# One step apart: an output projection, a diagonal product and a module gate moved inside a selective-scan loop

## The chip, the core and the metric

The kernel runs on one core of a Trainium2 chip, in one launch. The metric is the device time in microseconds (us). The engines are named as in the profile: PE is the matmul engine (PEld is its weight load), DVE the vector engine, ACT the scalar engine, POOL the GpSimd engine, and SP the engine that issues most DMAs.

## What is computed

The whole program is two layers over an input of 4 x 256 x 32 x 32: a hybrid layer (four small Mamba modules, a gated convolution, attention), then attention and a mixture of 16 experts. Only the Mamba part of the first layer is touched here. In short form, for each batch element and each of four groups of 64 channels:

```
xc  = layernorm(x)                        # 64 channels of this group, 1024 positions
u,z = xc @ inw.T ; u = silu(conv(u))      # 128 channels each
dt  = softplus(...) ; h_t = exp(dt*A)*h + dt*u*B ; y_t = <h_t, C_t>     # 16 states per channel
y   = y + u * D
xm  = (y * silu(z)) @ outw.T + skip_scale * xc
...
g   = sigmoid(two small convolutions over all 256 channels of xm)       # one gate per group
xg  = g * xm
```

`u * D`, `skip_scale * xc`, the product with `outw` and the gate `g` are the pieces that the change moves.

## The kernel before

There are 4 batch elements `b` and 4 modules `nb`, so 16 pairs, and I call each pair a block `n = 4b + nb`. A block holds 128 channels x 16 states = 2048 recurrences of 1024 positions. They are processed in 16 steps `j`, 128 recurrences at a time, so the scan loop has 256 steps `t = 16n + j` (plus 4 to drain). All work is written into one loop over `t`, and inside it the order of the source is the order on every engine: nothing is rescheduled. The position of a piece of work is therefore the step in which the loop calls it. The change's own short description says "block" for what is called a step here.

In every step the loop emits, in this order:

- DVE: `dBu * B` (L876, in place in PSUM) and the scan itself (L879). They form the recurrence's input and output `hs`.
- POOL: `hs * C` (L880).
- In step 3, ACT copies the finished `pY` of the block before (`gated`, L485).
- PE: `select(t+2)` (L817) spreads `dt*u` for two steps later into one of **two** `dBu` PSUM buffers. It can run only when scan `t` has finished with that buffer, and DVE needs it two steps later.
- PE: `add_up(t-3)` sums `hs * C` over the states into `pY`. In the first two and last two positions of a block this is L828 (4 matmuls). Between them, every second step does two steps at once with L835 (8 matmuls that run in pairs). It also holds the product `u * D` as a matmul with a diagonal (`ddiag`, L841), one half of the columns in each of two steps. `add_up` also releases `hs`, which has six buffers.
- SP and ACT: fetch `dt` of four steps ahead (L805), and the exponential of it for three steps ahead (`decay`, L810).
- Then the pieces of the block's surroundings, each in its own step: the front of the next block (`project` L403, `silu` L407, `project_dt` L414, `exps`, `rest` L425/L426, `log`, `dt_out` L432 to L435, `part1`/`part2` L439 to L445, the two `spread`s L461/L463, DMAs `parts_out` L449 and `turn` L456), `times_gate` of the block before (L488, POOL), `project_out` (L498/L499), `store` (L504, ACT), `gate` (L476/L478), and the module gate of the batch element before (`module_gate`, L513 to L530).

All of these surrounding pieces pass through **one** PSUM buffer of 128 x 1024, called `mm` (the function `big()`), so each waits until the one before has been read out of it. In step order `mm` belongs to `project_dt`, `exps` and `log` (steps 0 to 5, released by L432 on DVE in step 5), `spread(0)` (6), `spread(1)` (7), `project_out` (8) to `store` (9), `gate` (9), in some blocks `module_gate` (10), and `project` and `silu` of the next block (11 to 15).

A matmul in float32 appears as two instructions of 512 columns; a half of 512 columns is therefore two, a full width of 1024 is four. `project_out` adds two products in one accumulation: `sdiag` (the diagonal of `skip_scale`) times `xc`, with the 64 rows of this module as contraction, and the output weights of the two modules of a pair times `u`, with 128 rows. Only the 64 output rows of this module are stored.

Of the kernel before, what the change touches and what calls it, by code (L numbers as in the profile page):

```python
# [13 lines left out]
ALU = mybir.AluOpType  # L14
# [4 lines left out]
N = HH * WW  # L19
# [4 lines left out]
NB, DM, DIN, DS, DTR, K = 4, 64, 128, 16, 4, 4  # L24
# [3 lines left out]
DB, XL = P // DS, K - 1  # L28
# [288 lines left out]
def body(tc, g, out):  # L317
    nc = tc.nc
    act, mm = nc.scalar.activation, nc.tensor.matmul
    ts, tt, stt = nc.vector.tensor_scalar, nc.vector.tensor_tensor, nc.vector.scalar_tensor_tensor  # L320
    HALVES = (slice(0, 512), slice(512, 1024))
# [4 lines left out]
    with pool("const", 1) as cp, pool("dram", 1, space=bass.MemoryType.DRAM) as drp, contextlib.ExitStack() as late:  # L326
# [16 lines left out]
        def V(name, j=0, n=1):  # L343
            return vec[:, VOFF[name] + j : VOFF[name] + j + n]
# [19 lines left out]
        XM = []  # L364
        for b in range(B):
            t = xmp.tile([P, CT, XL + N + 1], F32, tag=f"xm{b}", name=f"xm{b}")
# [4 lines left out]
        order = [(nb, b) for b in range(B) for nb in range(NB)]  # L371
        NBLK = NJ * len(order)
        with pool("mconst", 1) as mc, pool("front", 1) as fp, pool("dts", 2, space=bass.MemoryType.DRAM) as dsp, pool(
# [8 lines left out]
            sdiag = mc.tile([P, P], F32, tag="sdiag", name="sdiag")  # L382

            def block(nb, b):
                q0 = (nb % 2) * DM
                return slice(q0, q0 + DM), XM[b][q0 : q0 + DM, nb // 2]

            def big():
                return mps.tile([P, N], F32, tag="mm", name="mm")
# [90 lines left out]
            def gated(n):  # L480
                u, pY, sz = (state[n][k] for k in ("u", "pY", "sz"))
                if n == len(order) - 1:
                    tt(u, pY, sz, ALU.mult)
                else:
                    nc.scalar.copy(u, pY)  # L485

            def times_gate(n):
                nc.gpsimd.tensor_tensor(state[n]["u"], state[n]["u"], state[n]["sz"], ALU.mult)  # L488

            def project_out(n):  # L490


                nb, b = order[n]
                rows_out, xb = block(nb, b)
                po = state[n]["po"] = big()
                two = m_out[:, nb // 2 * 2 : nb // 2 * 2 + 2].rearrange("p n d -> p (n d)")
                for h in HALVES:
                    mm(po[:, h], sdiag[rows_out, :], xb[:, XL + h.start : XL + h.stop], start=True, stop=False)  # L498
                    mm(po[:, h], two, state[n]["u"][:, h], start=False, stop=True)  # L499

            def store(n):
                nb, b = order[n]
# [3 lines left out]
            def module_gate(b, step):  # L506

                q12 = late_gate[0]  # L510
                if step == 0:
                    if b == 0:
                        nc.gpsimd.memset(q12, 0.0)  # L513
                    p = big()
                    for h in HALVES:
                        for k in range(CT):
                            mm(p[:96, h], qdw[:, k, :], XM[b][:, k, XL + h.start : XL + h.stop], start=k == 0, stop=k == CT - 1)
                    for j in range(3):
                        rows_j = slice(32 * j, 32 * j + NB)
                        act(  # L520
                            q12[rows_j, 2 - j : 2 - j + N], p[rows_j], AF.Identity,
                            bias=V("qdw_b")[rows_j] if j == 1 else 0.0, scale=1.0,
                        )
                else:
                    k, t = step - 1, late_gate[1]
                    p = big()
                    for h in HALVES:
                        mm(p[:, h], qpw[:, k * P : (k + 1) * P], q12[:, 1 + h.start : 1 + h.stop], start=True, stop=True)
                    act(t, p, AF.Sigmoid, bias=V("qpw_b", k), scale=1.0)
                    nc.gpsimd.tensor_tensor(XM[b][:, k, XL : XL + N], XM[b][:, k, XL : XL + N], t, ALU.mult)  # L530

            late_gate = []
            state = {}
            with pool("scan", 6) as sp, pool("yps", 1, space=PSUM) as yps, pool("dps", 2, space=PSUM) as dps, pool("lnA", 1) as wp:
# [10 lines left out]
                for b in range(B - 1, B):  # L545
                    t = wp.tile([P, CT, N], F32, tag=f"xs{b}", name=f"xs{b}")
# [251 lines left out]
                def which(t):  # L798

                    return t % NJ // 8 * 8 + t % 2 * 4 + t % 8 // 2  # L800

                def fetch(t):
                    if t < NBLK:
                        dAs[t] = sp.tile([P, N], F32, tag="dA", name="dA", bufs=5)
                        nc.sync.dma_start(out=dAs[t], in_=state[t // NJ]["ds"][which(t)].unsqueeze(0).to_broadcast([DS, DB, N]))  # L805

                def decay(t):
                    if t < NBLK:
                        c = order[t // NJ][0] * NJ + which(t)
                        act(dAs[t], dAs[t], AF.Exp, scale=aneg[:, c : c + 1])  # L810

                def select(t):
                    if t < NBLK:
                        j = which(t)
                        dBus[t] = dps.tile([P, N], F32, tag="dBu", name="dBu")
                        for h in HALVES:
                            mm(dBus[t][:, h], pick[:, j % 4], state[t // NJ]["U"][:, j // 4, h], start=True, stop=True)  # L817

                def add_up(t):
                    if not 0 <= t < NBLK:  # L820
                        return
                    r, p, j = state[t // NJ], t % NJ, which(t)
                    if p == 0:
                        r["pY"] = yps.tile([P, N], F32, tag="y", name="pY")
                    if not 2 <= p < 14:
                        hs = hss.pop(t)
                        for h in HALVES:
                            mm(r["pY"][:, h], strip[:, P - DB - j * DB : 2 * P - DB - j * DB], hs[:, h], start=p == 0, stop=p == NJ - 1)  # L828
                    elif p % 2:

                        two = {which(u): hss.pop(u) for u in (t - 1, t)}
                        for h in HALVES:
                            for c, hs in two.items():
                                q, i = c // 4, c % 4
                                mm(  # L835
                                    r["pY"][32 * q : 32 * q + 32, h], strip[:, P - DB - i * DB : P - i * DB + 32 - DB], hs[:, h],
                                    start=False, stop=False,
                                )
                    if p in (1, 2):
                        h = HALVES[p - 1]  # L840
                        mm(r["pY"][:, h], ddiag[:, order[t // NJ][0]], r["u"][:, h], start=False, stop=False)  # L841

                fronts = [front(n) for n in range(1, len(order))]
# [26 lines left out]
                with tc.manual_schedule():  # L870
                    for t in range(NBLK + 4):
                        n, j = t // NJ, t % NJ
                        if t < NBLK:
                            r = state[n]
                            dBu = dBus.pop(t)
                            tt(dBu, dBu, r["B"], ALU.mult)  # L876

                            hs = hss[t] = sp.tile([P, N], F32, tag="hs", name="hs")
                            nc.vector.tensor_tensor_scan(hs, dAs.pop(t), dBu, 0.0, ALU.mult, ALU.add)  # L879
                            nc.gpsimd.tensor_tensor(hs, hs, r["C"], ALU.mult)  # L880
                        if j == 3 and n > 0:
                            gated(n - 1)
                        select(t + 2)
                        add_up(t - 3)
                        fetch(t + 4)
                        decay(t + 3)
                        for ahead in (1, 2):
                            if n + ahead < len(order):
                                for i, step in fronts[n + ahead]:
                                    if i == j - (ahead - 1) * NJ:  # L890
                                        step()
                        for i, step in behind:
                            if i == t:
                                step()
                        if 0 < n < len(order) and j == 4:
                            times_gate(n - 1)
                        if n > 0 and j == (8 if n < len(order) else 3):
                            project_out(n - 1)
                        if n > 0 and j == (9 if n < len(order) else 3):
                            store(n - 1)  # L900
                        if n < len(order) and j == 9:
                            gate(n)
                        if n >= NB and j == 10 and n % NB < 3:
                            module_gate(n // NB - 1, n % NB)

# [10 lines left out]
        with pool("sets", 1) as wp, pool("work", 1) as kp, pool("ps2", 1, space=PSUM) as ps:  # L918
# [988 lines left out]
            for i in range(B * NT + 2):  # L1907
                b, unit = i // NT, (i - 2) // HT
# [25 lines left out]
        with pool("fin", 3) as fp, pool("rows", 1) as yp, pool("pfin", 4, space=PSUM) as pf:  # L1934
# [5 lines left out]
            for u in range(2 * B):  # L1940
                b, half = u // 2, u % 2
# [20 lines left out]
```

## Time and profile before

| what | us |
|---|---|
| median of 3 runs | 3153.95 (3152.73 to 3158.89) |
| the profiled execution, its own time | 3144.65 |
| its span, first to last instruction | 3142.9 |
| end of the first and of the last scan, from the span's start | 103.0 and 1114.5 |
| DVE busy between 115 and 1115 us | 905.8 |
| PE busy there | 822.2 |
| POOL busy there | 777.5 |
| ACT busy there | 625.5 |

The profiled execution is 9.3 us below the median of the timed runs, so a sum over its rows is a difference to be taken from either, not an absolute time. The scan loop is about a third of the program. What follows (attention, routing, experts) needs the loop's result: the first of it starts in the trace right after the last `store`. The granted PE clock over the span is 0.939 of full speed.

In timelines a row is: start in us, duration in us, engine, line, operation, output<-inputs, shape, number of instructions merged, and in brackets the idle time of the engine before the row with what ended it. In the table of waits a row is: who waited <- for whom: total us, times, longest us.

### The profile page before, as it was taken

Reading aid. Unit: us, or ns where it says so; the run is one execution under the profiler, and the core shown is the slowest. Engines: PE = TensorE matmul, PEld = TensorE weight load, DVE = VectorE, ACT = ScalarE, POOL = GpSimd, SP = SyncE. Lnnn points to the kernel's source line nnn. Section 1 sums busy time; section 2 is a strip of 40 time slices with the busy share of each in tenths; the row PEclk is TensorE's granted clock in tenths of the full one; section 3 lists DMA queues with packets and bytes.
Section 4 is the critical chain, followed back from the end, with each engine's and each line's share of the span. In section 5 each row is a group of like instructions: output and inputs, shape, how many; then the busy total and the mean of one; then the engine's idle time right before and its main releaser. Section 6 shows DMA issues by size and latency. Waiting matters only on the chain. (4 is left out here: it accounts for less than half of the span.)

```text
span 3142.9 us, 38694 instructions
## 1 busy us (share of the span) xinstructions
PE 2741.2 (87%) x15244; PEld 1555.1 (49%) x15244; DVE 2033.9 (65%) x2324; ACT 1531.9 (49%) x2090; POOL 1289.5 (41%) x806
## 2 busy tenths in 40 slices
PE   6788888888888779999889899989879999899996
PEld 3322222222222225555545555555545666789996
DVE  5799988989989965655785496567365555511112
ACT  3666656666667414455744673576443333211111
POOL 0687877778768710000010010001024434666662
PEclk8799999999999889999989999999989999899998
DMA  3576666656756620000000000000000002456445
GB/s 132 136 176 166 173 159 165 167 153 173 178 153 164 169 87 1 1 1 1 28 1 1 28 1 1 1 15 1 14 1 7 14 14 78 124 148 168 90 125 165
DMA packets 92872, 265.50 MB, mean 84 GB/s; under 512 B 18182, under 2 KB 36086, under 8 KB 89360
## 3 DMA queue, kind: packets, MB, share of 16 engines
q1 hardware_dynamic: 64000, 198.46, 23.6%
q0 software_dynamic: 26512, 60.35, 7.5%
q10 hardware_dynamic: 2176, 4.19, 0.3%
q8 instruction: 121, 1.98, 0.3%
q14 instruction: 63, 0.52, 0.1%
HBM read 291.70 MB, written 42.80 MB: 106 GB/s over the span
## 5 line engine op out<-in xcount | busy, mean ns | idle before, releaser
L880 POOL TENSOR_TENSOR hs<-hs,bc 128x1024 f32<-128x1024 f32 x256 | 600.9, 2357 | 178.6 <-DVE hs L879 176.8
L879 DVE TENSOR_TENSOR_SCAN hs<-dA,dBu 128x1024 f32<-128x1024 f32 x256 | 585.5, 2287 | 45.5 <-PE pY L835 15.6
L1170 DVE TENSOR_REDUCE nm<-s 128x1 f32<-128x1024 f32 x256 | 301.5, 1219 | 187.4 <-PE s L1165 186.6
L1175 ACT ACTIVATE pr<-s,nm 128x1024 f32<-128x1024 f32 x256 | 285.2, 1115 | 234.9 <-DVE nm L1170 232.7
L1189 PE MATMUL k<-const,pr 128*128 128x128 f32 x2048 | 298.8, 289 | 81.0 <-ACT pr L1175 47.9
L876 DVE TENSOR_TENSOR dBu<-dBu,bc 128x1024 f32<-128x1024 f32 x256 | 310.6, 1213 | 50.9 <-PE dBu L817 50.4
L1239 POOL TENSOR_TENSOR b<-b 128x1024 f32<-128x1024 f32 (+1 forms) x15 | 30.3, 2019 | 761.5 <-ACT b L1235 751.8
L810 ACT ACTIVATE dA<-dA,aneg 128x1024 f32<-128x1024 f32 x256 | 285.9, 1144 | 106.2 <-DMA dA<-ds 97.2
L1189 PEld LDWEIGHTS k<-const,pr 128*128 128x128 f32 x2048 | 230.1, 145 | 182.2 <-ACT pr L1175 77.8
L1165 PE MATMUL s<-b,b 32*128 32x512 f32 x1024 | 286.6, 653 | 1.7 <-ACT pr L1175 1.7
L817 PE MATMUL dBu<-U,pick 96*128 96x512 bf16 x512 | 160.6, 396 | 138.2 <-DVE hs L879 137.7
L1195 ACT COPY pT<-k 128x512 f32<-128x512 f32 x320 | 172.8, 594 | 139.5 <-PE k L1189 137.6
L1837 PE MATMUL s<-pT,b 128*128 128x128 f32 x1920 | 233.8, 279 | 6.2 <-DMA b<-we,intse 5.6
L1837 PEld LDWEIGHTS s<-pT,b 128*128 128x128 f32 x1920 | 229.1, 194 | 12.4 <-issue 3.5
L835 PE MATMUL pY<-hs,const 128*32 128x512 f32 x768 | 222.5, 709 | 0.0
L817 PEld LDWEIGHTS <-pick 96*128 96x128 bf16 x512 | 40.2, 98 | 322.0 <-issue 174.7
L1841 DVE TENSOR_TENSOR pT<-pT,s 128x512 f32<-128x512 f32 x72 | 49.3, 685 | 227.2 <-ACT pT L1840 227.2
L1195 DVE COPY pT<-k 128x512 f32<-128x512 f32 x192 | 131.1, 686 | 70.1 <-PE k L1189 69.0
L1209 PE MATMUL k<-pT,b 128*32 128x128 f32 x4096 | 147.8, 289 | 7.5 <-ACT pT L1195 4.3
L1209 PEld LDWEIGHTS k<-pT,b 128*32 128x32 f32 x4096 | 111.3, 115 | 80.7 <-issue 43.9
L1165 PEld LDWEIGHTS s<-b,b 32*128 32x128 f32 x1024 | 103.1, 191 | 88.4 <-issue 75.3
L403 PE MATMUL mm<-xm,m_cu 64*128 64x512 f32 x240 | 125.7, 646 | 14.9 <-ACT xs L520 8.5
(470 smaller groups left out, 4560.0 us busy)
## 6 DMA issues: line engine op xcount, KB each, us to landing
dA<-ds SPq DMA_DIRECT2D x256, 512.0 KB, 4.7
dq<-parts SPq DMA_DIRECT2D x15, 768.0 KB, 6.1
U<-dq SPq DMA_DIRECT2D x45, 256.0 KB, 6.1
ds<-dt SPq DMA_DIRECT2D x16, 512.0 KB, 3.0
b<-x SPq DMA_DIRECT2D x4, 1024.0 KB, 6.9
acc<-pr SPq DMA_DIRECT2D x8, 512.0 KB, 8.1
xm<-x SPq DMA_DIRECT2D x4, 1024.0 KB, 4.9
tokens<-pr SPq DMA_DIRECT2D x8, 512.0 KB, 2.9
```

The source lines that it names most:

```text
L810: act(dAs[t], dAs[t], AF.Exp, scale=aneg[:, c : c + 1])
L835: mm(r["pY"][32 * q : 32 * q + 32, h], strip[:, P - DB - i * DB : P - i * DB + 32 - DB], hs[:, h], start=False, stop=False,)
L876: tt(dBu, dBu, r["B"], ALU.mult)
L879: nc.vector.tensor_tensor_scan(hs, dAs.pop(t), dBu, 0.0, ALU.mult, ALU.add)
L880: nc.gpsimd.tensor_tensor(hs, hs, r["C"], ALU.mult)
L1165: mm(S[i][:, HALVES[h]], qT[rr, qt * P : (qt + 1) * P], kT[rr, HALVES[h]], start=True, stop=True)
L1170: "DVE", 1220, lambda i=i, u=u: nc.vector.tensor_reduce(nms[u], S[i], AX.X, ALU.max, negate=True),
L1175: "ACT", 1330, lambda i=i, u=u, hd=hd: act(prs[u % 4], S[i], AF.Exp, bias=nms[u], scale=1.0, accum_out=rss[b % 2][:, k, qt, hd : hd + 1]), ...
L1189: nc.tensor.transpose(bank.t[:, j * P : (j + 1) * P], prs[u][:, c0 : c0 + P], ident)
L1195: lambda dst=dst, bank=bank, on_act=on_act: (nc.scalar.copy if on_act else nc.vector.tensor_copy)(dst, bank.t),
L1209: mm(bank.t[i * HD : (i + 1) * HD, 0:P], v[:, 4 * jh + j, hd * HD : (hd + 1) * HD], pTs[m][jh][:, i, j * P : (j + 1) * P], start=j == 0, s ...
L1837: mm(p12[:, a, c], wbufs[w][:, o : o + P], xT[:, k], start=k == 0, stop=k == CT - 1)
```

## The change

- `project_out(n, i)` does one half of the columns: half 0 in step 8, half 1 in step 9. Before, both halves were in step 8.
- The skip product contracts over all 128 rows of the pair (`sdiag` whole, `XM[b][:, nb // 2]` whole) instead of the module's 64. The rows that aren't stored get values that nobody reads.
- The two halves of `u * D` (L841) move from steps 4 and 5 to steps 3 and 4.
- `gate(n)` moves from step 9 to step 10.
- The module gate's three PE/ACT stages move from step 10 of the blocks with `n % 4` = 0, 1, 2 to step 5 of those with `n % 4` = 1, 2, 3. Its POOL product (L530) is taken out of them and placed in step 8 of the blocks with `n % 4` = 2 and 3.

```diff
-            def project_out(n):
+            def project_out(n, i):
                 nb, b = order[n]
-                rows_out, xb = block(nb, b)
-                po = state[n]["po"] = big()
+                if i == 0:
+                    state[n]["po"] = big()
+                po, h = state[n]["po"], HALVES[i]
                 two = m_out[:, nb // 2 * 2 : nb // 2 * 2 + 2].rearrange("p n d -> p (n d)")
-                for h in HALVES:
-                    mm(po[:, h], sdiag[rows_out, :], xb[:, XL + h.start : XL + h.stop], start=True, stop=False)
-                    mm(po[:, h], two, state[n]["u"][:, h], start=False, stop=True)
+                mm(po[:, h], sdiag, XM[b][:, nb // 2, XL + h.start : XL + h.stop], start=True, stop=False)
+                mm(po[:, h], two, state[n]["u"][:, h], start=False, stop=True)
...
                     act(t, p, AF.Sigmoid, bias=V("qpw_b", k), scale=1.0)
-                    nc.gpsimd.tensor_tensor(XM[b][:, k, XL : XL + N], XM[b][:, k, XL : XL + N], t, ALU.mult)
+
+            def module(b, k):
+                x = XM[b][:, k, XL : XL + N]
+                nc.gpsimd.tensor_tensor(x, x, late_gate[1], ALU.mult)
...
-                    if p in (1, 2):
-                        h = HALVES[p - 1]
+                    if p in (0, 1):
+                        h = HALVES[p]
                         mm(r["pY"][:, h], ddiag[:, order[t // NJ][0]], r["u"][:, h], start=False, stop=False)
...
-                        if n > 0 and j == (8 if n < len(order) else 3):
-                            project_out(n - 1)
-                        if n > 0 and j == (9 if n < len(order) else 3):
+                        last = n == len(order)
+                        for i in range(2):
+                            if n > 0 and j == (3 if last else 8 + i):
+                                project_out(n - 1, i)
+                        if n > 0 and j == (3 if last else 9):
                             store(n - 1)
-                        if n < len(order) and j == 9:
+                        if not last and j == 10:
                             gate(n)
-                        if n >= NB and j == 10 and n % NB < 3:
-                            module_gate(n // NB - 1, n % NB)
+                        if n > NB and j == 5 and n % NB > 0:
+                            module_gate(n // NB - 1, n % NB - 1)
+                        if n > NB and j == 8 and n % NB > 1:
+                            module(n // NB - 1, n % NB - 2)
```

## The prediction

> **What bounds the kernel now.** I read the costliest groups first, then who DVE waits for inside the scan loop (180 to 1115 us, blocks 1 to 15), then timelines of two blocks.
>
> ```profile
> L879 DVE TENSOR_TENSOR_SCAN hs<-dA,dBu 128x1024 f32<-128x1024 f32 x256 | 585.5, 2287 | 45.5 <-PE pY L835 15.6
> L876 DVE TENSOR_TENSOR dBu<-dBu,bc 128x1024 f32<-128x1024 f32 x256 | 310.6, 1213 | 50.9 <-PE dBu L817 50.4
> ```
>
> The pair takes 3.50 us and repeats every 3.54 where nothing is late; steps 4 and 6 also carry L425 and L432 (1.2 each). That is 58.8 us for a block. The loop's end opens all later phases, so only DVE's idle time can be won:
>
> ```profile
> DVE dBu L876 <- PE dBu L817: 44.1, 23, 4.0
> DVE hs L879 <- PE pY L835: 15.1, 19, 2.5
> DVE hs L879 <- ACT dA L810: 3.0, 4, 0.8
> DVE hs L879 <- DVE dBu L876: 0.6, 2, 0.5
> ```
>
> Together 62.8 us, nearly all for PE. Spacing of scan ends says where: some 31 us in steps 11 and 12 of almost every block, some 32 us in steps 13 to 15 of the blocks that hold a module gate. A block without one, number 7, on PE and then DVE:
>
> ```profile
> 578.78 0.81 PE L817 MATMUL dBu<-U,pick 96*128 96x512 bf16 x2 [3.11 <-DVE hs L879]
> 579.52 3.35 PE L835 MATMUL pY<-hs,const 128*32 128x512 f32 x8
> ...
> 588.23 1.91 PE L835 MATMUL pY<-hs,const 128*32 128x512 f32 x8
> 590.07 1.12 PE L498 MATMUL mm<-xm,sdiag 64*128 64x512 f32 x2
> 591.13 1.13 PE L499 MATMUL mm<-u,m_out 128*128 128x512 f32 x2
> 592.18 1.12 PE L498 MATMUL mm<-xm,sdiag 64*128 64x512 f32 x2
> 593.24 1.13 PE L499 MATMUL mm<-u,m_out 128*128 128x512 f32 x2
> 594.20 0.60 PE L817 MATMUL dBu<-U,pick 96*128 96x512 bf16 x2
> ```
> ```profile
> 590.48 2.29 DVE L879 TENSOR_TENSOR_SCAN hs<-dA,dBu 128x1024 f32<-128x1024 f32 x1
> 594.83 1.23 DVE L876 TENSOR_TENSOR dBu<-dBu,bc 128x1024 f32<-128x1024 f32 x1 [2.07 <-PE dBu L817]
> ```
>
> The select of step 9 (594.20) stands behind L835 and the whole `project_out` of step 8, 5.97 us from 588.23, and DVE needs it at 592.76. The same L835 takes 1.91 or 3.35 us: the granted clock halved for one stretch after PE's 3.11 us of idleness. Block 10, with the half rate elsewhere, loses 0.5 instead of 2.07. The module gate of block 8, on PE and DVE:
>
> ```profile
> 660.95 3.68 PE L517 MATMUL mm<-xm,qdw 128*96 128x512 f32 x8
> 664.46 0.60 PE L817 MATMUL dBu<-U,pick 96*128 96x512 bf16 x2
> 667.87 3.77 PE L403 MATMUL mm<-xm,m_cu 64*128 64x512 f32 x4 [2.82 <-ACT xs L520]
> ```
> ```profile
> 672.65 1.23 DVE L876 TENSOR_TENSOR dBu<-dBu,bc 128x1024 f32<-128x1024 f32 x1 [3.91 <-PE dBu L817]
> ```
>
> It comes when PE is already late, holds `mm` through three ACT copies, stalls L403 and with it the next select, and the idleness halves the clock.
>
> **What the Trainium skill says.** "TensorE: Matmul & The Clock Gate", part 1: the PE clock falls to half after an idle window of about 3.4 us, on a free-running grid. The trace agrees and sharpens it: in slices of 3.41 us, 27 of the 28 full-rate slices that half rate followed had PE busy for at most 1.56 us, and only one other was under 1.57. Its section on LDWEIGHTS says that the number of rows doesn't set the load's time; here 64-row and 128-row matmuls take 642 and 645 ns (L498, L499), so 128 rows cost nothing. "TensorEngine Tiling (Array Packing)", Key Properties: a change of tiling mode drains the engine. `project_out` alternates 64 and 128 rows at 1.055 us a pair; pairs in L461 (all 128 rows) average 0.92. That agrees, without proving the cause.
>
> **The change part by part.** I lay one block end to end with these durations: select 0.52, L835 1.84, four full-row matmuls 1.83 (L461), four of 64 rows 1.91 (L476, L403). Zero is the end of scan 5; unstalled scans end at 4.58, 8.03, 11.57, 15.09, 18.63, then every 3.54. Select of step t must be done 0.07 before scan t+1 ends.
>
> *Projection in two halves, gate one step later.* Step 6: select 4.63, L835 to 6.99, spread to 8.82. Step 7: select to 9.34; `mm` free at 10.0 (ACT copy 1.01); spread to 11.88. Step 8: select to 12.40, L835 to 14.24, half 0 to 16.07 (16.35 if pairs stay at 1.055). Step 9: select to 16.6, due 18.56, **1.96 to spare, where half 1 of the old form cost the stall**; half 1 to 18.4, `store` to 19.5. Step 10: select to 19.2 (due 22.10), L835 to 21.0, gate to 23.0. Step 11: select to 23.5 (due 25.64), `mm` free after ACT's silu at 24.1, L403 to 26.1. Step 12: select 26.6 (due 29.18), L835 to 28.4 (due about 30.4, `hs`), L403 to 30.3. Step 13: select 30.85 (due 32.72), L403 to 32.8. Step 14 starts on time. The narrowest margin is 1.87. Nothing is added: two pairs per half, one accumulation kept open across a step in a buffer that nobody else gets. Removed: the stall, about 31 us.
>
> *D products.* Two matmuls (0.86) go from step 5 to 4 and from 4 to 3. Step 3 is then 0.52 + 1.72 + 0.86 = 3.10 of 3.54, step 4 the same: covered. They queue behind L828's wait for ACT's copy of the old `pY` (L485; PE waited 7.0 us for it in the whole loop, 6 times); with `select` ahead of them the cost is 0 to 0.4 a block, and I take 0. But step 5 is left with a select alone: 4.0 us idle until 4.63, where the old one was 3.1, so half rate in step 6 is certain in blocks without a module gate.
>
> *Module gate.* 9 stages leave step 10 (31 to 32 us come back) and enter step 5, where PE has those 4.0 us. `mm` is free when L432 ends, 1.2. L517's 8 matmuls end at 4.75, so select 6 is 0.1 late; three L520 (1.01, 1.11, 1.01) hold `mm` to 7.95; L461 wants it at 7.0. That is 0.95 late against margins of 1.9. Behind L520 on ACT stand `decay(9)` and the cast L439: the cast ends at 10.1 instead of 7.0, L440 on POOL at 12.2 instead of 9.1, second spread free at 14.3. POOL's chain (`hs*C` 2.36 a step, 1.18 to spare) is about 4 us behind and, with the product of step 8 (another 2.36), catches up by step 13; L835 first misses `hs` only at about 5 behind. L528's stages hold `mm` to 5.5 with a table load (1.28), no delay. Block 5 also puts the memset of `q12` (L513, 0.95) before L520: 1.0 more, so it may stall, 0.3 to 2; I take 1.0. In the 9 blocks the 1.8 to 3.7 us of PE work in step 5 lift every slice above 1.57, so the half rate there should go.
>
> *Queues.* No DMA is added or moved; SP's `parts_out` waits for L445, at worst 17.8, ahead of its turn at 18.6. Tail: the last `project_out` is one piece as before, shorter by 0.4.
>
> *What stays.* Blocks 1 to 4, 8, 12: half rate in step 6 costs 1.6 (block 7 against 10) against margins of 1.87 or less after a small catch-up; 0 to 0.75 each, take 0.4, 2.4. Block 5: 1.0. Blocks 9 and 13: 0.4 together. Sum: 62.8 + 0.4 - 3.8 = 59.4. The profiled execution would go from 3144.65 to about 3085; it lay 9.3 under the median, so I take the difference from the median: **3095**.
>
> **Rivals.**
> 1. *Margins are eaten (0.24).* Steps 8 to 14 are now nearly solid PE work. If a second half-rate slice falls there, or pairs stay slow, each block keeps about 1.7: 15 x 1.7 = 25, gain 37, **3117**. For: margins of 1.9 against a price of 1.6. Against: no slice there falls under 1.57 busy.
> 2. *The stall only moves (0.03).* Select was late for another reason, such as ACT's decay waiting for its DMA (up to 4.9 us). DVE waited only 3.0 us for ACT; 3154.
> 3. *Slower (0.04).* `mm` at step 5: ACT may reach the gate's copies late, and both spreads, projection, gate and L403 queue behind that one buffer. To cancel 62.8 us it must cost 7 us in each of 9 blocks, so with 1.9 of margin `mm` must come free near 16, 9 us after its due time. ACT's longest wait for a `dA` transfer was 4.9, which gives 1.2 + 4.9 + 3.1 = 9.2. From 16 it decides; at 18 it gives 9 x 9 = 81 - 63, **3172**.
>
> **How the numbers follow.** Likeliest, 0.69: 3095, own range 3088 to 3102 (residue 0 to 9, 3 for the medians). A measurement tells about 0.2%, 6 us. Rival 1 reaches 3122; below, the gain can't pass 63.2, but timed medians lie up to 9 above a profiled run, so 3083. Faster 0.69 + 0.24 = 0.93, same 0.03, slower 0.04.
>
> **What would show it.** Right: DVE's wait for L817 falls from 44 to under 5 and for L835 under 3; last scan near 1055; L498 shows 128 rows and pairs near 0.92; L835 of step 6 at 3.3 us in blocks 1 to 4, 8 and 12 but 1.9 in the nine others; L403 no longer waits for L520. Wrong: DVE waits of 1.5 us in steps 9 to 15 of most blocks (rival 1), or L461 waiting on L520/L529 by more than 3 us (rival 3).

## The result, and the profile after

The changed kernel takes 3103.73 us (median of 4, 3101.09 to 3104.79) against 3154.76 for the kernel before on the same chip: ratio 0.9835, 95% interval 0.9818 to 0.9852, 51 us faster. The forecast was 3095 (3083 to 3122), 59 us faster. The direction and most of the amount are right; 8 us are missing.

In the profiles the scan loop, from the end of the first scan to the end of the last, goes from 1011.5 to 963.1 us, which is 48.4. The rest of the program has its own scatter: from the last scan to the end it takes 2027.5 to 2035.8 us over the twelve profiles of this study, although nothing there was changed. I therefore compare profiles by the loop, and whole kernels by the timed runs.

The costliest groups of the changed kernel, with the same columns as before (L882 and L879 are the old L879 and L876):

```profile
L882 DVE TENSOR_TENSOR_SCAN hs<-dA,dBu 128x1024 f32<-128x1024 f32 x256 | 585.4, 2287 | 38.9 <-PE pY L838 9.9
L879 DVE TENSOR_TENSOR dBu<-dBu,bc 128x1024 f32<-128x1024 f32 x256 | 309.9, 1210 | 11.1 <-PE dBu L820 11.1
```

The waits of DVE in its scan loop, from 170 us on:

```profile
DVE hs L882 <- PE pY L838: 9.4, 8, 2.1
DVE dBu L879 <- PE dBu L820: 5.0, 8, 0.9
DVE hs L882 <- DVE dBu L879: 0.9, 4, 0.5
DVE e L425 <- ACT mm L422: 0.2, 1, 0.2
```

The wait for the select (L820) fell from 44.1 us to 5.0, about as forecast (under 5). The wait for L838 (the old L835) fell only from 15.1 to 9.4, where under 3 was expected. Block 7 shows why the first one fell. PE rows of the changed kernel:

```profile
567.43 1.91 PE L838 MATMUL pY<-hs,const 128*32 128x512 f32 x8
569.27 1.13 PE L498 MATMUL mm<-xm,sdiag 128*128 128x512 f32 x2
570.24 1.02 PE L499 MATMUL mm<-u,m_out 128*128 128x512 f32 x2
571.09 0.60 PE L820 MATMUL dBu<-U,pick 96*128 96x512 bf16 x2
571.53 1.02 PE L498 MATMUL mm<-xm,sdiag 128*128 128x512 f32 x2
572.39 1.02 PE L499 MATMUL mm<-u,m_out 128*128 128x512 f32 x2
573.66 0.59 PE L820 MATMUL dBu<-U,pick 96*128 96x512 bf16 x2 [0.26 <-DVE hs L882]
```

The select of step 9 now stands behind one half only. It ends at 571.69 and is due at 573.54: 1.85 us to spare, where the hand schedule had 1.96. The next select, at 573.66, waits for DVE, so PE has caught up by step 10, as the schedule said.

What is left can be read from block 8, on PE and then on DVE:

```profile
635.98 1.99 PE L476 MATMUL mm<-xm,m_in 64*128 64x512 f32 x4
637.89 0.60 PE L820 MATMUL dBu<-U,pick 96*128 96x512 bf16 x2
639.07 3.57 PE L403 MATMUL mm<-xm,m_cu 64*128 64x512 f32 x4 [0.58 <-ACT sz L478]
642.58 1.04 PE L820 MATMUL dBu<-U,pick 96*128 96x512 bf16 x2
643.54 3.19 PE L838 MATMUL pY<-hs,const 128*32 128x512 f32 x8
```
```profile
643.65 1.23 DVE L879 TENSOR_TENSOR dBu<-dBu,bc 128x1024 f32<-128x1024 f32 x1 [0.73 <-PE dBu L820]
646.93 2.29 DVE L882 TENSOR_TENSOR_SCAN hs<-dA,dBu 128x1024 f32<-128x1024 f32 x1 [2.05 <-PE pY L838]
```

L403 takes 3.57 us instead of 1.98 and L838 3.19 instead of 1.91: the clock is at half rate from 639.3 to 646.1, and DVE loses 2.8 us. In the loop the recorded clock changes only at points that lie 3.41 us or a multiple of it apart; one such stretch of 3.41 us is called a slice, and a block is called hit when half rate follows the slice that holds its gate. That happens in blocks 1, 4, 8 and 13. Together it is 11.1 of the 15.8 us that blocks 1 to 15 still lose against unstalled spacing (63.9 before, by the same count).

### The profile page after: what moved, and what is told of

Read it like the earlier page. It is cut to its first block, busy times and chain, and to the rows that moved or that the text cites. A ratio compares the mean times of both kernels' runs of the same rounds, so it can differ in the third digit from the quotient of the medians.

```text
span 3099.3 us, 38699 instructions
## 1 busy us (share of the span) xinstructions
PE 2719.9 (88%) x15244; PEld 1553.9 (50%) x15244; DVE 2031.6 (66%) x2324; ACT 1529.4 (49%) x2090; POOL 1289.5 (42%) x806
## 3 DMA queue, kind: packets, MB, share of 16 engines
q8 instruction: 121, 1.98, 0.3%
## 5 line engine op out<-in xcount | busy, mean ns | idle before, releaser
L882 DVE TENSOR_TENSOR_SCAN hs<-dA,dBu 128x1024 f32<-128x1024 f32 x256 | 585.4, 2287 | 38.9 <-PE pY L838 9.9
L879 DVE TENSOR_TENSOR dBu<-dBu,bc 128x1024 f32<-128x1024 f32 x256 | 309.9, 1210 | 11.1 <-PE dBu L820 11.1
L820 PE MATMUL dBu<-U,pick 96*128 96x512 bf16 x512 | 161.1, 397 | 121.5 <-DVE hs L882 121.2
L838 PE MATMUL pY<-hs,const 128*32 128x512 f32 x768 | 214.6, 686 | 0.0
L820 PEld LDWEIGHTS <-pick 96*128 96x128 bf16 x512 | 39.9, 98 | 298.1 <-issue 172.3
L1216 PEld LDWEIGHTS k<-pT,b 128*32 128x32 f32 x4096 | 111.7, 115 | 80.7 <-issue 44.1
L403 PE MATMUL mm<-xm,m_cu 64*128 64x512 f32 x240 | 124.9, 643 | 8.1 <-ACT sz L478 8.1
```

What stands on the lines that cost most here:

```text
L838: mm(r["pY"][32 * q : 32 * q + 32, h], strip[:, P - DB - i * DB : P - i * DB + 32 - DB], hs[:, h], start=False, stop=False,)
L1216: mm(bank.t[i * HD : (i + 1) * HD, 0:P], v[:, 4 * jh + j, hd * HD : (hd + 1) * HD], pTs[m][jh][:, i, j * P : (j + 1) * P], start=j == 0, s ...
```

## The experiments

For each kernel the loop is that of one profile, and the ratio is to the kernel before, timed beside it on the same chip.

### What halves the clock in step 12: rows or a gap

Theory A: a matmul that contracts over 64 rows counts as about half activity. Theory B: the 0.58 us gap ahead of L403 counts, or the offset of the slices alone. The gate's weights get zeros for the other module's rows, so the same product runs over 128 rows (the one line of the edit that does the product):

```diff
-                    mm(p[:, h], m_in[rows_in, nb // 2, DIN:], xb[:, XL + h.start : XL + h.stop], start=True, stop=True)
+                    mm(p[:, h], m_z[:, nb, :], XM[b][:, nb // 2, XL + h.start : XL + h.stop], start=True, stop=True)
```

> The gate product (L476 before) contracts over 128 rows, the weights of the other module's 64 rows being zero; all else as in the changed kernel. Theory A, rows: the activity that decides the clock counts a matmul of 64 rows at about half, so the slice around the gate and the first L403 (2.84 us busy, 2.2 of it with 64 rows) passes for light and the half rate follows. Then the half rate at steps 12 and 13 goes in blocks 1, 4, 8 and 13, the four waits of 2.7 us in step 14 go, the last scan ends near 1055 instead of 1065.5 and the time is near 3093. Theory B, gap: the 0.55 us in which L403 waits for the PSUM buffer is what makes the slice light. The gap stays, so the waits stay: last scan 1063 to 1068, time near 3104.

Measured: 3090.18 us, ratio 0.9817 (0.9792 to 0.9843); last scan at 1055.3, loop 953.3; no half rate at step 12 or 13. Busy time of the gate's slice and the two after it in block 8 of the changed kernel, then of the gate's slice and the one after it in block 4 of this kernel; columns are window, its length, PE, PEld, DVE, ACT and POOL busy, granted clock, DMA share and GB/s:

```profile
635.90:639.30 3.40, 2.82 (x9) 1.01 (x8) 3.27 (x3) 2.66 (x4) 2.94 (x2) 1.00 0.78 204
639.30:642.70 3.40, 3.40 (x5) 0.85 (x5) 3.27 (x3) 3.39 (x4) 2.35 (x1) 0.50 1.06 212
642.70:646.10 3.40, 3.40 (x8) 0.56 (x9) 1.45 (x2) 0.86 (x1) 2.35 (x1) 0.50 1.05 231
```
```profile
393.12:396.53 3.41, 2.73 (x9) 1.17 (x8) 3.28 (x3) 2.67 (x4) 2.91 (x2) 1.00 0.77 187
396.53:399.94 3.41, 3.41 (x12) 0.87 (x13) 3.28 (x2) 3.40 (x4) 2.35 (x1) 1.00 1.05 209
```

PE rows of this kernel there (L484, L829, L411 and L847 are the gate, the select, the projection and the sum):

```profile
393.14 1.99 PE L484 MATMUL mm<-xm,m_in 128*128 128x512 f32 x4
394.96 0.60 PE L829 MATMUL dBu<-U,pick 96*128 96x512 bf16 x2
396.24 1.98 PE L411 MATMUL mm<-xm,m_cu 64*128 64x512 f32 x4 [0.68 <-ACT sz L486]
398.15 0.60 PE L829 MATMUL dBu<-U,pick 96*128 96x512 bf16 x2
```

A slice of the clock's grid began 0.02 us before the gate here, as in block 13 of the changed kernel. PE was busy for 2.73 of its 3.41 us, less than in block 8 there (2.84 over the whole slice), and the gap was longer (0.68), yet full rate followed. That speaks against B. But only one slice of this run began at such an offset, so I repeated both kernels side by side. Half rate has not left this kernel altogether: three slices between steps 15 and 0, busy for 2.0 to 2.7 us, with 1.5 to 2.0 us of that in L411's 64-row matmuls, were still followed by it.

> The changed kernel once more, beside the next two, so that they are compared on one chip. The clock's slices of 3.41 us run freely, so another execution meets other offsets. The light slice is one that begins 0.02 to 0.12 us before the gate's first matmul (blocks 13, 8, 4, 1 of the first profile, all followed by two slices of half rate; block 2 at 0.17 was not). If that is the rule, this profile has half rate at step 12 in just those blocks whose slice begins in that band and the last scan is 1055 to 1067, about 2.7 us per block hit.

Measured: 3100.44 us, ratio 0.9854 (0.9837 to 0.9871), loop 957.2. Two blocks were hit: block 2 at 0.06, inside the band, and block 1, whose slice began 0.05 **after** the gate's first matmul. The band was stated too narrow on that side; block 3 at 0.14 was spared.

> The gate product over 128 rows once more. Theory A, rows: no half rate at steps 12 and 13 in any block, at whatever offset the slices begin; scan loop 952 to 955 us from first to last scan, 5 to 10 us under the changed kernel beside it. Theory B, offsets only: the first run was free of it because only one of its slices fell in the band of 0.02 to 0.12 us; another run has hits at the changed kernel's rate, 2.7 us each.

Measured: 3088.09 us, ratio 0.9811 (0.9796 to 0.9826), loop 953.0. The intervals of the two don't overlap: 12 us between the medians. (The loops differ by 4 only; the profiled execution of the changed kernel, 3086.62, was the fastest of its five.)

Over all profiles with the gate in step 10, a slice began between 0.05 us after and 0.12 us before the gate in 15 blocks with 64 rows and in 4 with 128 rows that have a projection behind the gate. Half rate followed in 15 of 15 and in 0 of 4. (In two of the 15, blocks 8 and 12 of the run `module_back` below, the slice was lighter for another reason, 2.30 us busy.) At these offsets the rows of the gate's matmul decide it. The traces say the same beyond the gate: over all twelve profiles, in blocks 1 to 15, half rate followed 21 of the 21 full-rate slices with PE busy for 1.8 to 2.4 us of which more than 1.2 us were 64-row matmuls, and none of the 383 with the same busy time of which less than 0.6 us was. How the hardware counts rows is not shown.

### What each part is worth

Module gate back at step 10, directly behind the gate (run `module_back`):

```diff
-                        if n > NB and j == 5 and n % NB > 0:
-                            module_gate(n // NB - 1, n % NB - 1)
-                        if n > NB and j == 8 and n % NB > 1:
-                            module(n // NB - 1, n % NB - 2)
+                        if n >= NB and j == 10 and n % NB < 3:
+                            module_gate(n // NB - 1, n % NB)
+                            if n % NB > 0:
+                                module(n // NB - 1, n % NB - 1)
```

> The module gate and its product go back to step 10 (behind the gate, which stays there), the rest of the change stays. If the parts add up as in the prediction, 32 us of waits come back: last scan near 1097, time near 3136. If the two-step projection left margins that swallow a gate stage, only the blocks with three ACT copies (4, 8, 12) still wait, 6 to 9 us each: last scan 1085 to 1092. By hand: behind the gate, L517 starts at 24.1 and the next select ends 2.7 us late, then L403 waits for three copies and the half rate follows, so 8 to 10 us in three blocks and 1 to 2 in six, 1090 to 1105.

Measured: 3164.14 us, ratio 1.0044 (1.0030 to 1.0057), last scan 1131.6, loop 1031.8. It is slower than the kernel before, beyond every expectation. PE rows of block 9, where I had counted 1 to 2 us and 8.7 were lost, then DVE:

```profile
729.40 1.99 PE L476 MATMUL mm<-xm,m_in 64*128 64x512 f32 x4
732.50 3.78 PE L528 MATMUL mm<-xs,qpw 96*128 96x512 f32 x4 [1.11 <-ACT sz L478]
736.07 1.06 PE L820 MATMUL dBu<-U,pick 96*128 96x512 bf16 x2
737.48 3.78 PE L403 MATMUL mm<-xm,m_cu 64*128 64x512 f32 x4 [0.35 <-ACT r L529]
```
```profile
737.17 1.23 DVE L879 TENSOR_TENSOR dBu<-dBu,bc 128x1024 f32<-128x1024 f32 x1 [4.33 <-PE dBu L820]
```

Three users of `mm` stand within two steps. Each waits for ACT to read the one before; the slice that begins at 729.09 has PE busy for 2.30 us, and four slices of half rate (13.7 us) follow it, which nearly double the time of what stands between DVE and its select. That the waits and the 64-row matmuls together made that slice light is argued from the rows, not tested apart.

Both halves of the projection back in step 8, gate in step 9:

```diff
-                            if n > 0 and j == (3 if last else 8 + i):
+                            if n > 0 and j == (3 if last else 8):
...
-                        if not last and j == 10:
+                        if not last and j == 9:
```

> Both halves of the projection are in step 8 again and the gate in step 9; the 128-row skip product, the D products and the module gate stay moved. Sum of parts as in the prediction: 31 us come back, last scan near 1096. The other theory: a stall of 2.1 in steps 11 and 12 was 0.5 of work and 1.6 of half rate from the idle step 5; the module gate now fills step 5 in nine blocks, and the 128 rows shorten the projection by 0.4 to 0.5, so at full rate the select is just in time. Then only the blocks with half rate in step 6 (1 to 4, 8, 12) wait, about 1.6 to 2 each, and the last scan is at 1065 to 1078.

Measured: 3116.48 us, ratio 0.9901 (0.9877 to 0.9925), last scan 1078.3, loop 978.3, with 22 us of waits in steps 11 and 12. That is the upper end of the second theory; the sum of parts (1096) is out. The agreement is partly luck: the blocks with half rate in step 6, which that theory named, hold 11.5 of the 22 us; blocks 5, 9, 13 and 15, which it left out, hold 9.6.

The kernel before with the module gate's move alone (the added lines are those of the change's diff):

> The kernel before, with only the module gate moved (stages to step 5, product to step 8); projection in one piece, gate in step 9, D products in steps 4 and 5, skip product over 64 rows. If the parts add up as in the prediction, 32 of the 63 us of waits go and the stalls of steps 11 and 12 stay at about 2.4 a block: scan loop near 980. The other theory: the stages in step 5 also keep the clock up in step 6 of nine blocks, and take 1.6 us from each of their stalls, 14 us more: scan loop 963 to 970.

Measured: 3115.66 us, ratio 0.9906 (0.9888 to 0.9924), loop 979.6, 31.9 less than before. Of this, 2.5 lie in block 0, where the edit changes nothing, so 29.4 belong to blocks 1 to 15; that is near the additive 32. The half rate in step 6 did leave the nine blocks, and blocks 6, 7 and 11 got back 1.6 us each in steps 11 and 12. But the others of the nine gained little there or lost more than before, and blocks 6 to 15 other than 8 and 12 kept 0.8 to 3.0 us each: of the further 14 us of the second theory, 3 came.

Read together: the module gate's move alone is worth about 30 us. The projection's split on top brings 16 to 22 more (979.6 to 963.1 or 957.2). Without the module gate's move, the loop with the split is 20 us longer than before. The two parts share `mm` and PE's idle time and cannot be priced apart.

### Small parts

D products back in steps 4 and 5 (`p in (1, 2)`):

> The products with D are in steps 4 and 5 again, the rest of the change stays. Prediction: they cost nothing in either place, last scan within 1.5 us of 1065.5; block 10 loses its 1.1 us in steps 3 and 4 since the product no longer follows the first sum there. Rival: the product fills step 5 and keeps the clock up in step 6 of blocks 1 to 4, 8 and 12 (idle 3.1 instead of 4.0 us), which would take away most half-rate stretches in step 6 and move the slices: last scan 2 us or more earlier.

Measured: 3093.56 us, ratio 0.9830 (0.9801 to 0.9858), loop 953.0. The prediction's band is missed: the last scan is at 1057.4, 8 us earlier than in the first profile of the changed kernel (but the second profile of that same kernel has 1056.5). The loop is shorter by what the rival named, but not for its reason: half rate around step 6 is still there in blocks 1 to 4, 8 and 12. What is absent is the hits at step 12; only block 8 had one that made DVE wait. Block 10 no longer waits in steps 3 and 4, but block 11 now does (0.8 us). The ratio lies inside the changed kernel's interval.

The skip product over 64 rows:

```diff
-                mm(po[:, h], sdiag, XM[b][:, nb // 2, XL + h.start : XL + h.stop], start=True, stop=False)
+                mm(po[:, h], sdiag[block(nb, b)[0], :], block(nb, b)[1][:, XL + h.start : XL + h.stop], start=True, stop=False)
```

> The skip product contracts over the module's 64 rows again, the rest of the change stays. Prediction: a pair of L498 and L499 goes back from 0.92 to 1.055 us, which is 0.13 to 0.27 us more PE work in steps 8 and 9 against margins near 1.9, so nothing on DVE: scan loop within what two profiles of the changed kernel gave (957 and 963 us). Rival from the clock: the four matmuls of 64 rows in steps 8 and 9 count half, slices there pass for light and the half rate falls into steps 9 to 11 in several blocks, 1.7 us each: loop 968 or more.

Measured: 3098.47 us, ratio 0.9845 (0.9828 to 0.9862), loop 957.2. The first half of the projection takes 1.82 us in the changed kernel (569.27 to 571.09) and 2.01 here between the same neighbours. It costs nothing on DVE, as predicted.

The POOL product in step 5 (`j == 5` in place of `j == 8` for `module`):

> The module gate's POOL product (L530 before) follows its sigmoid in step 5 instead of step 8, the rest of the change stays. By the hand schedule POOL waits for the sigmoid until 4.2 to 5.5, so the product ends at 6.6 to 7.9 and POOL runs 1 to 3 us behind until step 8, which delays L440 and the second spread by as much in six blocks. If the margins of steps 8 to 13 hold that, the loop stays at 955 to 964 us. If step 8 was needed for the product, the six blocks (5 to 11 and 13 to 15 without those of three copies) wait 1 us or more each: loop 965 to 975.

Measured: 3111.08 us, ratio 0.9888 (0.9871 to 0.9904), loop 961.1. In the profile the six blocks that hold a product lose 0.8 us (block 11), 1.2 (block 14) and otherwise nothing; both losses are in steps 3 and 4, ahead of the product. Another 8.4 us stand at step 14 of blocks 4, 8 and 12. But the median of the timed runs is 12 us above that of the 64-row kernel, which ran beside it. Whether the product's place costs that, or more hits at step 12 in the unprofiled runs, stays open.

### A version that beats both

Gate over 128 rows, D products in steps 4 and 5, and the clearing of `q12` out of block 5:

```diff
-                    if b == 0:
-                        nc.gpsimd.memset(q12, 0.0)
...
+                        if t == NJ + 12:
+                            nc.gpsimd.memset(late_gate[0], 0.0)
```

> Three edits to the changed kernel: gate over 128 rows, products with D back in steps 4 and 5, and the clearing of the module gate's input (L513, 0.95 us on POOL) moved from step 5 of block 5 to step 12 of block 1. Expected: block 5 loses its 1.2 us of waits in steps 9 and 10, no block waits at steps 3 and 4, none at step 14; DVE waits 1 to 3 us in blocks 1 to 15 and the scan loop takes 951 to 953 us. If the products with D matter in either place, or the clearing was not the reason for block 5's wait, the loop stays at 953 to 956.

Measured: 3082.34 us (3080.88 to 3087.22), ratio 0.9799 (0.9784 to 0.9814), loop 951.1. It is faster than both kernels; against the 128-row gate alone (3088.09, timed beside it) the intervals overlap. Block 5 waits 0.0. Two expectations failed: DVE waits 4.2 us, not 1 to 3, and blocks 8 and 10 wait 1.1 and 1.2 us in steps 3 and 4, after two half-rate slices in step 0. So the D products were not the cause of block 10's 1.2 us in the changed kernel either. The twelve profiles point to the clock again: two half-rate slices in a row begin about step 0 of a block from 1 to 14 in 14 places, each behind a slice with PE busy for 2.0 to 2.7 us of which 1.4 to 2.0 were the 64-row matmuls of L403. In all 14 the block waits 0.8 to 1.2 us in steps 3 and 4, and no other of these blocks waits there.

## Why the prediction was right, and where it fell short

- **The bound.** That only DVE's waits for PE in the scan loop could be won held: the loop lost 48.4 us in the first profile and 54.3 in the second, and later phases didn't change beyond their scatter.
- **The schedule.** Its margins were right within 0.1 us (1.96 against 1.85 in step 9; 1.87 against 1.78 in step 13, where the select ends at 585.93 and is due at 587.71). The stalls of steps 11 and 12, 31 us, are 0.4.
- **Module gate.** 32 us, nearly confirmed alone (29.4 where the edit acts, 31.9 with block 0). Block 5's memset: 1.0 taken, 1.3 measured, and 0.0 with the memset moved. Blocks 9 and 13: 0.4 taken, nothing measured apart from step 14.
- **Half rate in step 6.** It is there in exactly blocks 1 to 4, 8 and 12 and gone in the other nine, as forecast. I took 2.4 us for its waits; they were 1.8 (steps 7 to 13 of those blocks).
- **Rows of the skip product.** The prediction set times of matmuls beside a statement on weight loads. The loads themselves take 184 ns over 64 rows (L498) and 188 over 128 (L499) in the trace before, so its conclusion that the added rows cost nothing stands.
- **The step that failed.** "Against: no slice there falls under 1.57 busy", the argument that held rival 1 down. The threshold came from slices in which few matmuls had 64 rows. The gate's new place puts it next to L403 in one slice, 2.84 us busy of which 2.2 are 64-row, and half rate followed. So neither an idle window nor a threshold of busy time, as the prediction read the clock, describes what these runs show. The term "what stays" was 3.8 and measured 15.8: 11.1 of the 12.0 too much stand in step 14 of blocks 1, 4, 8 and 13, and 1.2 in block 10. With the gate over 128 rows the ratio is 0.9811 and 0.9817; the forecast was 3095/3153.95 = 0.9813. How many blocks are hit is a matter of where the slices fall: four in the first profile, two in the second. The warning stood in the trace of the kernel before, ahead of the 180 us from which the prediction counted. Two slices there were followed by half rate with PE busy for 2.39 and 2.51 us, 1.6 and 1.75 us of it in L403 (columns as in the tables of slices above):

```profile
159.21:162.62 3.41, 2.39 (x8) 0.71 (x8) 3.28 (x3) 1.20 (x2) 2.92 (x2) 1.00 0.90 207
162.62:166.03 3.41, 3.41 (x9) 0.63 (x6) 3.28 (x3) 1.15 (x1) 2.16 (x2) 0.50 1.08 213
172.86:176.27 3.41, 2.51 (x8) 0.74 (x7) 3.28 (x3) 2.76 (x3) 3.41 (x2) 1.00 0.58 159
176.27:179.68 3.41, 3.41 (x10) 0.56 (x8) 3.28 (x3) 3.40 (x4) 3.31 (x2) 0.50 0.63 153
```

- **Rival 1** had the mechanism (a second half-rate slice in steps 8 to 14), not the amount: 2.8 us in 4 blocks, not 1.7 in 15. Block 5 shows it in small: in the nine runs with the module gate in step 5 and the memset before it, the block waits 1.3 us in steps 9 and 10, or 2.3 to 2.8 where a half-rate slice falls around step 8 (six of the nine).
- **Rivals 2 and 3** are out: the waits didn't move to ACT, and L461 didn't wait long for the module gate in step 5 (4.9 us in all, at most 2.9).
- **Additive parts.** The sum treated projection and module gate as 31 and 32 that don't touch. Together they came out near that, but the experiments show a strong interaction: either part without the other leaves 15 to 75 us of loop time behind.

## What to carry to other kernels

Lay the critical engine's instructions end to end between two deadlines before moving work: the margin, not the sum of busy time, tells what fits where, and a hand schedule from profile rows was good to 0.1 us here. Work moved into an engine's idle stretch can pay twice if that stretch let the clock fall, but here the second gain was mostly lost again in other steps (3 of 14 us came). When matmuls with few rows are brought together, check the clock of the slices after them; padding the gate with zero weights cost no time (1.98 us for its four matmuls either way) and removed the half rate behind it, though not the one behind other slices full of 64-row matmuls.

## What the hardware showed that was not expected

- A slice of 3.41 us with PE busy for 2.84 us was followed by half rate when 2.2 us of it were 64-row matmuls, and one with 2.73 us was not when the gate had 128 rows.
- The effect hangs on less than 0.2 us: slices that began between 0.05 us after and 0.12 us before the gate were hit, at 0.06 after and 0.14 before not. A kernel with few such hits in one profile isn't free of them.
- Once at half rate, a slice filled with L403's 64-row matmuls (3.3 us of 3.41) was followed by a second half-rate slice; in `module_back` the stretch was 13.7 us in blocks 5, 9 and 13, and 20.5 us from step 13 of block 4 on.
